# The last token block's schedule, resident first-layer expert weights and an incremental last table in a one-layer attention and mixture-of-experts kernel

## The chip, the cores and the metric

One NeuronCore of one Trainium2 chip runs the whole kernel. The time is the device time of one execution, in microseconds; a lower time is better.

## The reference

For x of 4 sequences of 1024 tokens and 256 channels, two residual steps are computed, all in f32.

```python
x = x + attn(layernorm(x))         # causal, 16 heads of 16, ALiBi slopes, projection
x = x + ffn(layernorm(x))
# ffn: attention over the 4 sequences at each position (16 heads), h = layernorm(u + attn_out)
probs = softmax(h @ router_w.T + router_b); assign = max(top_2(probs))       # 1 of 7 experts
out = gelu(h @ w1[assign].T + b1[assign]) @ w2[assign].T + b2[assign]
ffn = layernorm(h + out)
```

Since the larger of the two best indices is taken, a token goes to one expert out of 1 to 7. The 4096 tokens are therefore sorted by expert into tiles of 128 rows, and each tile is computed with one expert's weights.

## The kernel before

`fast_layer` (line 573) writes its own order of work. There is one thread of emission; each engine then executes its instructions in the order in which they were emitted, so whatever is emitted between two steps of a chain stands between them in the queues.

**Attention.** Units of a sequence and one or two 128-token blocks run in rounds. One round scores four heads (L884 on TensorE, exp on ScalarE at L892) and weighs the values (L925). Around each pair of rounds the loop offers slots: `E_slot` for VectorE work and `D_slot` for TensorE work, in which the other coroutines may take a step. Fixed jobs are entered for a slot with `at_E` and `at_D`.

**Fronts.** A position block i of 128 positions times 4 sequences goes through `front(i, ...)` (line 1421), a generator of steps: "E" steps need VectorE, "D" steps TensorE, "P" steps wait for a step on GpSimd. Its steps are layernorm statistics (`u`), the transpose to `ut`, the q/k/v projection (L1469), the 4 x 4 scores on VectorE (`pr`, `sc`, L1490 and L1491), exp on ScalarE (L1501), `tot`, the weighted values (L1510), for the last block their sum and transpose on TensorE (`ctp`, L1533), the output projection (`ao`, L1556), the second layernorm (`rstd_h`, GpSimd, L731), the router and its choice (`hot`), the write of h to DRAM (`rows`), and the rank of each token among its expert's tokens (`place`, L1614). There are 8 fronts; fronts 6 and 7 are the last, and front 7 can start only when attention has ended.

`take_E` and `take_D` (lines 1817 and 1833) walk the list `running` (at most two fronts, plus a table builder put ahead of them) and let each take at most one E step in a slot; after an E step a D step has to wait for one slot more.

**Tables.** After six fronts `tabulate_first` sorts the first 3072 tokens into 18 full tiles. After all eight, `tabulate_rest` (line 1179) splits the ranks, counts the tokens per expert (`counts`, L1106 and L1115), finds each token's tile, spreads the last two fronts' places into one-hot tiles (`at_places`, L1099), sums them on TensorE (`who`, L1266) and writes the row numbers of the other 20 tiles.

**Tiles.** A tile (class `Tile`, line 1638) is gathered by an indirect DMA on GpSimd (L1647). Its expert's first weights, 256 KB, are loaded by a DMA on SyncE whose address comes from the table (L1663, 8 buffers). Then come three stages, one per `tile_step`: transposes and a ScalarE copy (`mtp`, L1674, `mt`, L1676); the first layer and gelu (`hid`, L1687, `ge`, L1696); the second layer, whose weights lie in SBUF whole as `w2` (`oe`, L1703 to L1708). Pairs of tiles are finished over the following steps: statistics on VectorE, `rstd_v` on GpSimd (L731), two VectorE operations a tile (L1720, L1723), and a scatter by an indirect DMA on GpSimd (L1730). PSUM holds three pairs of `oe`.

**The tail.** After attention (line 1985) the loop at line 2052 offers three E slots and one D slot in an iteration with a `tile_step` between each two. While a front is under way, `tile_step` does nothing if at most `HELD_BACK` = 6 tiles are left, or if the PE cost booked for tiles is above the VectorE cost booked.

```python
        if queue or running and part.placed < NT:
            if experts.left() <= HELD_BACK or busy["PE"] > busy["DVE"]:
                return
            busy["PE"] += TILE_PE
            busy["DVE"] += TILE_DVE
        experts.fetch()
        experts.advance()
```

Of the kernel before, what the change touches and what calls it, by code (L numbers as in the profile page):

```python
# [37 lines left out]
P = 128  # L38
# [3 lines left out]
G = H // 4  # L42
# [24 lines left out]
N_W1 = 8  # L67
HELD_BACK = 6
TILE_PE, TILE_DVE = 2.6, 1.6
# [503 lines left out]
def fast_layer(ctx: ExitStack, tc: tile.TileContext, odd, x, wq, wk, wv, wp, w_in, w_out, w_r,  # L573
# [146 lines left out]
    def norm_stats(src, n, name, tag=""):  # L720
        stats = small.tile([P, B, 6], F32, tag="stats" + tag, name=f"stats_{name}")
        mv = small.tile([P, B, 2], F32, tag="mv" + tag, name=f"mv_{name}")
        rstd = small.tile([P, B], F32, tag="rstd" + tag, name=f"rstd_{name}")
        for i in range(n):
            nc.vector.bn_stats(stats[:, i], src(i))
            nc.vector.bn_aggr(mv[:, i], stats[:, i])
        nc.vector.tensor_scalar(rstd[:, :n], mv[:, :n, 1], EPS, None, ALU.add)
        return mv, rstd

# [334 lines left out]
    class Routing:  # L1064
# [6 lines left out]
        def prepare(self):  # L1071
# [4 lines left out]
            self.firsts = numbered("firsts", [P, N_COLUMNS], [[P, N_COLUMNS]])  # L1076
# [7 lines left out]
            )  # L1084

# [18 lines left out]
        def counts(self, n):  # L1104
            pm = bank(f"counts{n}")
            nc.tensor.matmul(pm[:, :E], ones_bf, self.so_far, start=True, stop=True)  # L1106
            count = keep.tile([P, E], F32, tag="count", name=f"count{n}")
            if n == 0:

                nc.vector.tensor_scalar(count, pm[:, :E], float(P - 1), None, ALU.subtract)  # L1110
            else:
                nc.vector.tensor_copy(count, pm[:, :E])
            some = N_COLUMNS if n else len(FIRST) * B
            full = keep.tile([P, E, N_COLUMNS], F32, tag="full", name=f"full{n}")[:, :, :some]
            nc.vector.tensor_tensor(  # L1115
                full, count.unsqueeze(2).to_broadcast([P, E, some]),
                self.firsts[:, :some].unsqueeze(1).to_broadcast([P, E, some]), ALU.is_gt,
            )
            tiles = const(f"tiles{n}", [P, E])
            nc.vector.tensor_reduce(tiles, full, AX.X, ALU.add)  # L1120
            return tiles

        def own_of(self, lo, hi):
            own = keep.tile([P, N_COLUMNS, E], F32, tag="own", name=f"own{lo}")[:, lo:hi]
            nc.vector.tensor_tensor(
                own, con(IOTA, E).unsqueeze(1).to_broadcast([P, hi - lo, E]),
                self.expert.rearrange("p k t -> p (k t)")[:, lo:hi].unsqueeze(2).to_broadcast(
                    [P, hi - lo, E]
                ), ALU.is_equal,
            )  # L1130
            return own
# [22 lines left out]
        def tabulate_first(self):  # L1154
# [3 lines left out]
            self.tiles = self.counts(0)  # L1158
# [8 lines left out]
            own = self.own_of(0, n)  # L1167
# [9 lines left out]
            yield from self.tabulate(0, 0, N_FIRST, nowhere, self.past(0, N_TILES, self.until, "whose0"))  # L1177

        def tabulate_rest(self):

            yield "D", 0.3
            lo, hi = len(FIRST) * B, N_COLUMNS
            self.split(lo, hi)
            tiles = self.counts(1)
# [6 lines left out]
            nc.vector.tensor_tensor(before, until, tiles, ALU.subtract)  # L1191
            found = const("found", [P, N_COLUMNS])
            self.looked_up(found, self.own_of(0, N_COLUMNS), before, "behind_of")
            nc.vector.tensor_tensor(found, found, self.by_128, ALU.add)

            mine, tile_of = found[:, :lo], self.tile_of[:, :lo]
            nc.vector.tensor_tensor(mine, mine, tile_of, ALU.subtract)
            nc.vector.tensor_tensor(mine, mine, self.late[:, :lo], ALU.mult)
            nc.vector.tensor_tensor(mine, mine, tile_of, ALU.add)
# [14 lines left out]
        def tabulate(self, n, first, end, tile_of, whose):  # L1214
# [11 lines left out]
            if n == 0:  # L1226
# [7 lines left out]
            nc.vector.tensor_scalar(  # L1234
                in_tile[:, :, 1], in_tile[:, :, 2], row_no, None, ALU.mult
            )
# [4 lines left out]
            who = table("who_f", [P, 3, n_tiles])  # L1241
            if n == 0:
                nc.vector.memset(who, 0.0)
# [17 lines left out]
            else:  # L1261
                at_place = late["at_place"]
                self.spread(at_place[-1], len(FIRST) * B, N_COLUMNS)
# [6 lines left out]
                self.whose = whose()  # L1270
                nc.vector.tensor_copy(who, pm)
# [10 lines left out]
            block, at_t = (table(name, [P, n_tiles], I32) for name in ("block", "at_t"))  # L1282
            nc.vector.tensor_scalar(  # L1283
                who[:, 2], who[:, 2], -float(NOWHERE), float(NOWHERE), ALU.mult, ALU.add
            )
            nc.vector.tensor_tensor(who[:, 1], who[:, 1], who[:, 2], ALU.add)
# [4 lines left out]
                who[:, 1], block, float(P), who[:, 1], ALU.mult, ALU.add  # L1291
            )
            nc.vector.scalar_tensor_tensor(
                out_rows, at_t, float(T), who[:, 1], ALU.mult, ALU.add
# [126 lines left out]
    def front(i, fact, more, last):  # L1421
# [6 lines left out]
        yield "E", 0  # L1428
# [71 lines left out]
        yield "E", 0  # L1500
        nc.scalar.activation(sc, sc, AF.Exp, scale=1.0 / math.sqrt(D))  # L1501
        yield "P", 1.6
# [44 lines left out]
        if not last:  # L1547
            if i < PC * (NC - 2):
                yield "E", 0
            yield "D", 2.4  # L1550
            ct = flipped(ctx_, "ct")
        yield "D", 1.8
        for t in range(B):
# [7 lines left out]
            nc.vector.tensor_tensor(u_[:, t], u_[:, t], pm, ALU.add)  # L1561
            if t == 1:
                yield "d", 1.8
        yield "E", 2.6

        taken = small.tile([P, B, E], F32, tag="taken", name=f"taken_{i}", bufs=2)
        nc.vector.tensor_copy(taken, u_[:, :, C:])
        mv, rstd = norm_stats(lambda t: u[:, t], B, f"h_{i}")
        yield "E", 0
# [36 lines left out]
        yield "E", 2.2  # L1606
        nc.vector.tensor_tensor(u, u, wide(row(G1)), ALU.mult)
# [3 lines left out]

        pm = bank(f"place_{i}")
# [12 lines left out]
        nc.vector.tensor_reduce(part.rank[:, i], rank, AX.X, ALU.add)  # L1625
        here = small.tile([P, E], F32, tag="here", name=f"here_{i}")
        nc.vector.tensor_reduce(here, hot.rearrange("p t e -> p e t"), AX.X, ALU.add)
        nc.vector.tensor_tensor(part.so_far, part.so_far, here, ALU.add)
        part.placed += 1
        if part.placed == len(FIRST):  # L1630
            running.insert(0, Running(part.tabulate_first()))
        if part.placed == NT:
            running.insert(0, Running(part.tabulate_rest()))
# [4 lines left out]
    class Tile:  # L1638
# [14 lines left out]
        def load_w1(self):  # L1653

            at = nc.values_load(
                self.table.at_w[0:1, self.j:self.j + 1], engines=[mybir.EngineType.SP],
# [6 lines left out]
            nc.sync.dma_start(  # L1663
                self.w1.rearrange("p c f -> p (c f)"),
                w1.rearrange("p e c f -> p (e c f)")[:, bass.ds(at + CC * C, CC * C)],
            )

        def stages(self):
# [7 lines left out]
            nc.scalar.copy(mt, pt)  # L1676
            yield
# [62 lines left out]
    class Experts:  # L1740
# [3 lines left out]
        def __init__(self):  # L1744
            self.step, self.fetched = 0, []
            self.n_fetched = self.n_finished = self.n_loaded = 0
            self.to_load = []
            self.under_way, self.done, self.finishing = [], [], []

        def fetch(self):  # L1750
            self.step += 1
            if tiles_to_do and self.n_fetched - self.n_finished < len(given):
# [4 lines left out]
                self.to_load.append(t)  # L1757
            while late and self.to_load and self.n_loaded - late["n_hid"] < N_W1:
                self.to_load.pop(0).load_w1()
                self.n_loaded += 1  # L1760
# [5 lines left out]
        def advance(self):  # L1766
            for it in list(self.finishing):
                n, stages = it
                if next(stages, self) is self:
                    self.finishing.remove(it)  # L1770
                    self.n_finished += n
# [384 lines left out]
```

## Time and profile before

| | us |
|---|---|
| median of 3 runs (869.72 to 882.4) | 875.27 |
| the profiled execution | 877.08 |
| its span, first to last instruction | 875.3 |
| TensorE busy in the span | 767.9 |
| VectorE busy | 535.7 |
| ScalarE busy | 393.1 |
| GpSimd busy | 253.1 |
| mean granted TensorE clock | 0.931 |

The span is on the profile's own clock, and 1.8 us of the execution lie outside it. A busy share is a mean over stages; the stages have different limits, so the stretches of the span have to be read one by one. "Idle before" an instruction is the engine's idle time ahead of it, with what ended it.

### The profile page before, as it was taken

Reading aid. Unit: us, or ns where it says so; the run is one execution under the profiler, and the core shown is the slowest. Engines: PE = TensorE matmul, PEld = TensorE weight load, DVE = VectorE, ACT = ScalarE, POOL = GpSimd, SP = SyncE. Lnnn points to the kernel's source line nnn. Section 1 sums busy time; section 2 is a strip of 40 time slices with the busy share of each in tenths; the row PEclk is TensorE's granted clock in tenths of the full one; section 3 lists DMA queues with packets and bytes.
Section 4 is the critical chain, followed back from the end, with each engine's and each line's share of the span. In section 5 each row is a group of like instructions: output and inputs, shape, how many; then the busy total and the mean of one; then the engine's idle time right before and its main releaser. Section 6 shows DMA issues by size and latency. Waiting matters only on the chain.

```text
span 875.3 us, 22574 instructions
## 1 busy us (share of the span) xinstructions
PE 767.9 (88%) x8981; PEld 576.8 (66%) x8981; DVE 535.7 (61%) x1275; ACT 393.1 (45%) x548; POOL 253.1 (29%) x359
## 2 busy tenths in 40 slices
PE   3998889998999999999999989989995997654993
PEld 2776667666666676666777767677773785543882
DVE  7334346339467773866687483793797668682454
ACT  1453436556555755655654554565461223100220
POOL 5432114212111211112121211121122448115685
PEclk9897979999999999999999999999996999865997
DMA  6445454524423333332554343244215563017550
GB/s 203 116 106 162 113 155 129 156 74 154 134 76 107 94 100 124 98 110 79 153 146 142 112 138 120 75 117 140 74 40 161 161 191 119 8 43 240 170 156 30
DMA packets 79108, 105.60 MB, mean 121 GB/s; under 512 B 19928, under 2 KB 59155, under 8 KB 78484
## 3 DMA queue, kind: packets, MB, share of 16 engines
q1 hardware_dynamic: 73548, 89.22, 34.7%
q0 software_dynamic: 4864, 14.16, 5.2%
q8 instruction: 73, 1.20, 0.6%
q10 hardware_dynamic: 584, 0.70, 0.3%
q14 instruction: 39, 0.32, 0.1%
HBM read 67.58 MB, written 35.12 MB: 117 GB/s over the span
## 4 chain that ended last, share of the span: by engine, by line
PE 58%; DVE 16%; issue 10%; DMA 6%; POOL 6%; ACT 2%; SPq 2%; POOLq 0%; DVEq 0%; ACTq 0%
PE sk L884 16%; PE pv L925 10%; PE qkvp L1469 8%; PE qkp L803 5%; PE op L991 3%; PE vp L824 3%; PE ao L1556 2%; DVE pv L1510 2%; POOL given L1647 2%; PE hid L1687 2%; POOL out_dram L1730 2%; PE oe L1703 2%; ACT p L892 2%; DVE pv L1543 1%; DMA yc<-y 1%
## 5 line engine op out<-in xcount | busy, mean ns | idle before, releaser
L892 ACT ACTIVATE p<-sk 128x1024 f32<-128x1024 f32 (+1 forms) x320 | 289.7, 937 | 210.2 <-PE sk L884 197.9
L902 POOL TENSOR_SCALAR_AFFINE_SELECT p<-p 128x512 f32<-128x512 f32 (+1 forms) x160 | 105.6, 663 | 453.2 <-ACT p L892 450.9
L884 PE MATMUL sk<-slots 32*128 32x128 f32 (+1 forms) x3456 | 217.8, 336 | 21.1 <-ACT p L892 16.2
L884 PEld LDWEIGHTS sk<-slots 32*128 32x128 f32 x3456 | 162.3, 191 | 77.7 <-ACT p L892 31.6
L925 PE MATMUL pv<-p,v 128*32 128x128 f32 (+1 forms) x3456 | 146.5, 318 | 0.0
L925 PEld LDWEIGHTS pv<-p,v 128*32 128x32 f32 x3456 | 98.2, 113 | 36.8 <-issue 7.8
L1469 PE MATMUL qkvp<-w_in,ut 128*128 128x512 f32 (+1 forms) x256 | 92.4, 495 | 0.2 <-DVE x L984 0.2
L803 PE MATMUL qkp<-xt,wqk 128*128 128x256 f32 x256 | 66.7, 406 | 0.7 <-ACT xt L793 0.7
L1469 PEld LDWEIGHTS qkvp<-w_in,ut 128*128 128x128 f32 x256 | 44.4, 190 | 31.1 <-issue 25.7
L803 PEld LDWEIGHTS qkp<-xt,wqk 128*128 128x128 f32 x256 | 50.2, 202 | 11.6 <-issue 2.0
L1687 PE MATMUL hid<-mt,w 128*128 128x128 f32 x304 | 49.9, 304 | 6.0 <-DMA w<-in_w_dram 3.0
L1476 DVE COPY qkv<-qkvp 128x264 f32<-128x264 f32 x28 | 12.1, 432 | 68.6 <-PE qkvp L1469 68.6
L1687 PEld LDWEIGHTS hid<-mt,w 128*128 128x128 f32 x304 | 44.2, 208 | 12.8 <-ACT mt L1676 5.6
L1647 POOL DMA_INDIRECT given<-rows,rows x38 | 42.2, 1109 | 33.2 <-DVE who_f L1283 14.4
L1696 ACT ACTIVATE ge<-hid 128x256 f32<-128x256 f32 x38 | 14.6, 383 | 82.6 <-PE hid L1691 44.2
L808 DVE COPY kq<-qkp 128x512 f32<-128x512 f32 x32 | 21.9, 686 | 46.6 <-PE qkp L803 46.3
L1478 ACT COPY qkv<-qkvp 128x512 f32<-128x512 f32 (+1 forms) x36 | 20.2, 562 | 48.5 <-PE qkvp L1469 45.2
L1510 DVE TENSOR_TENSOR pv<-qkv,sc 128x1024 f32<-128x1024 f32 x32 | 39.6, 1241 | 3.9 <-PE ctp L1533 3.7
L1703 PE MATMUL oe<-w,ge 128*128 x152 | 41.8, 400 | 0.1
L1730 POOL DMA_INDIRECT out_dram<-o,out_rows x38 | 39.4, 1037 | 6.9 <-issue 6.9
L1490 DVE TENSOR_TENSOR pr<-qkv 128x1024 f32<-128x1024 f32 x32 | 39.9, 1246 | 0.0
L991 PE MATMUL op<-wp,yc 128*128 128x256 f32 x124 | 34.6, 421 | 5.9 <-DVE yc L979 5.8
(259 smaller groups left out, 1003.9 us busy)
## 6 DMA issues: line engine op xcount, KB each, us to landing
slots<-k SPq DMA_DIRECT2D x128, 80.0 KB
w<-in_w_dram SPq DMA_DIRECT2D x38, 256.0 KB
k<-kq SPq DMA_DIRECT2D x32, 256.0 KB
y<-yt SPq DMA_DIRECT2D x24, 256.0 KB
v<-v SPq DMA_DIRECT2D x20, 288.0 KB
v<-v SPq DMA_DIRECT2D x4, 1152.0 KB
x<-in_x_dram SPq DMA_DIRECT2D x16, 256.0 KB
rows<-x SPq DMA_DIRECT2D x32, 128.0 KB
```

The lines of the kernel that those rows point to most:

```text
L803: nc.tensor.matmul(pm[:, k * W:(k + 1) * W], wqk[:, k, cc, half * P:(half + 1) * P], xt[:, cc], start=cc == 0, stop=cc == CC - 1,)
L884: nc.tensor.matmul(ps[h // 2][:, h % 2, width:to], kt[rows_, kb * P:(kb + 1) * P], qt[rows_, off:], start=True, stop=True,)
L892: nc.scalar.activation(pt[:, :, :width], ps[pair][:, :, :width], AF.Exp, scale=1.0 / math.sqrt(D))
L902: nc.gpsimd.affine_select(blocks, blocks, pattern=[[0, 2], [0, size], [1, P]], compare_op=ALU.is_ge, fill=0.0, base=0, channel_multiplier=-1,)
L925: nc.tensor.matmul(pv[h * S:(h + 1) * S, off:], vt[:, kb, at:at + S], pts[h // 2][:, h % 2, at_p:to], start=r == 0 and k == 0, stop=own an ...
L991: nc.tensor.matmul(pm[:, i * C:(i + 1) * C], yc[:, cc, i * P:(i + 1) * P], wp_sb[:, cc], start=cc == 0, stop=cc == CC - 1,)
L1469: nc.tensor.matmul(pq, ut[:, cc, t * P:(t + 1) * P], w_in_sb[:, cc, lo:hi], start=cc == 0, stop=cc == CC - 1,)
L1510: nc.vector.tensor_tensor(pr.rearrange("p s (h d) -> p s h d", d=D), qkv[:, :, 2 * C:3 * C].rearrange("p s (h d) -> p s h d", d=D), sc[:, ...
L1647: nc.gpsimd.indirect_dma_start(out=self.hx, out_offset=None, in_=t.rows_of, in_offset=bass.IndirectOffsetOnAxis(ap=t.rows_[:, self.j:self. ...
L1687: nc.tensor.matmul(ph[:, fc], self.w1[:, cc, fc * P:(fc + 1) * P], mt[:, cc], start=cc == 0, stop=False,)
L1703: nc.tensor.matmul(self.v, ge[:, fc], late["w2"][:, bass.ds(at + fc * C, C)], start=fc == 0, stop=False,)
L1730: ins = nc.gpsimd.indirect_dma_start(out=out.rearrange("t n c -> (t n) c"), out_offset=bass.IndirectOffsetOnAxis(ap=t.table.out_rows[:, t. ...
```

## The change

1. The last block's front is put at the head of `running` as `alone=True`. In the tail a coroutine takes all its E steps in a row in one slot, and front 7 may take its D step in the slot right after an E step. Steps that only issue to GpSimd or ScalarE become "N" steps, which end a row. In the last front the second layernorm's statistics are taken within the `ao` loop.
2. Tile steps are emitted by credit: each slot adds its E cost and 1.0, and a tile step costs 2.6, while more than `HELD_BACK` = 4 tiles wait and front 7 is not near its end. Two of these four are emitted, without finishing, ahead of the table, then six gathers.
3. The last four jobs of attention units of the last chunk, and the start of its fronts, are entered one or two E slots earlier. The last E slot of attention gives one step only. `project_slots` comes ahead of the weights' loads.
4. `w1` is loaded whole (1.75 MB, like `w2`) once; `copy_w1` reads the tile's expert number into a ScalarE register and copies 128 x 512 f32 from SBUF to SBUF on ScalarE, into 3 buffers.
5. `counts_all` is computed beside the last `place`; tiles per expert come from a shift instead of a comparison with 32 thresholds; `prepare_rest` does the part of the last table that concerns fronts 0 to 6 ahead of time; `in_tile`'s row plane is made by ScalarE.

```diff
-N_W1 = 8
-HELD_BACK = 6
-TILE_PE, TILE_DVE = 2.6, 1.6
+N_W1 = 3
+HELD_BACK = 4
+TILE_PE, STEP = 2.6, 1.0
...
+        def count_all(self, hot):
+            self.all = bank("counts_all")[:, :E]
+            for k, of_one in enumerate([self.so_far] + [hot[:, t] for t in range(B)]):
+                nc.tensor.matmul(self.all, ones_bf, of_one, start=k == 0, stop=k == B)
...
+        def prepare_rest(self, stage):
+
+            n = len(FIRST) * B
+            if stage == 0:
+
+                tile_of, late_ = self.tile_of[:, :n], self.late[:, :n]
+                nc.vector.tensor_tensor(
+                    self.own[:, :n], self.own[:, :n],
+                    late_.unsqueeze(2).to_broadcast([P, n, E]), ALU.mult,
+                )
+                by = const("by_late", [P, n])
+                nc.vector.tensor_tensor(by, self.by_128[:, :n], tile_of, ALU.subtract)
+                nc.vector.tensor_tensor(by, by, late_, ALU.mult)
+                nc.vector.tensor_tensor(tile_of, tile_of, by, ALU.add)
+            else:
+                self.split(n, n + B)
+                self.found_first(n, n + B)
+                nc.vector.tensor_copy(self.tile_of[:, n:n + B], self.by_128[:, n:n + B])
+                self.spread(late["at_place"][-1][:, :B], n, n + B)
 
         def tabulate_rest(self):
 
-            yield "D", 0.3
-            lo, hi = len(FIRST) * B, N_COLUMNS
+            lo, hi = N_COLUMNS - B, N_COLUMNS
+            whole = keep.tile([P, E], I32, tag="count", name="whole_all")
+            nc.vector.tensor_scalar(whole, self.all, float(P - 1), None, ALU.add)
+            nc.vector.tensor_single_scalar(whole, whole, 7, op=ALU.logical_shift_right)
+            tiles = const("tiles1", [P, E])
+            nc.vector.tensor_copy(tiles, whole)
             self.split(lo, hi)
-            tiles = self.counts(1)
...
-        def load_w1(self):
+        def copy_w1(self):
 
             at = nc.values_load(
-                self.table.at_w[0:1, self.j:self.j + 1], engines=[mybir.EngineType.SP],
+                self.table.at_w[0:1, self.j:self.j + 1], engines=[mybir.EngineType.Activation],
...
-            nc.sync.dma_start(
-                self.w1.rearrange("p c f -> p (c f)"),
-                w1.rearrange("p e c f -> p (e c f)")[:, bass.ds(at + CC * C, CC * C)],
+            nc.scalar.copy(
+                self.w1.rearrange("p c f -> p (c f)"), late["w1"][:, bass.ds(at, CC * C)]
             )
...
             nc.scalar.copy(mt, pt)
+            self.copy_w1()
             yield
...
-            if it.kind in ("E", "P") and it.slot < slot[0] - (it.kind == "P"):
+            was = it.slot
+            while it.kind in ("E", "N", "P") and was < slot[0] - (it.kind == "P"):
                 if cost and cost + it.cost > most:
-                    continue
+                    break
...
+                if it.kind != "E" or not (it.alone or most > E_SLOT):
+                    break
...
-                    if it.slot >= slot[0] - (it.was == "E"):
+                    if it.slot >= slot[0] - (it.was == "E" and not it.alone):
...
-    w2_sb = const("w2", [P, E - 1, CC, C], into=tail)
-    for g in range(2, G):
-        normalise(g)
-    load_sums(last_unit)
-    for lo, hi in ((1, 3), (3, 5), (5, E)):
-        nc.sync.dma_start(w2_sb[:, lo - 1:hi - 1], w2[:, lo:hi])
+    w1_sb, w2_sb = (const(name, [P, E - 1, CC, C], into=tail) for name in ("w1", "w2"))
+    for sb, src in ((w1_sb, w1), (w2_sb, w2)):
+        for lo, hi in ((1, 3), (3, 5), (5, E)):
+            nc.sync.dma_start(sb[:, lo - 1:hi - 1], src[:, lo:hi])
...
-    queue.append(front(NT - 1, fact, 1, True))
+    fetching.clear()
+    running.insert(0, Running(front(NT - 1, fact, 1, True), True))
...
+    def tile_step(finish=True):
+        experts.fetch()
+        experts.advance(finish)
...
+    while queue or running:
+        for take in (lambda: E_slot(k, 99.0), lambda: 0.0 * D_slot(p, 99.0)):
+            credit = min(credit, TILE_PE - STEP) + take() + STEP
+            while credit >= TILE_PE and experts.waiting() > HELD_BACK and "near" not in held:
+                tile_step()
+                credit -= TILE_PE
+        if part.placed == NT - 1 and not prepared:
+            prepared = True
+            part.prepare_rest(1)
+        k, p = k + 1, p + 1
+    for _ in range(HELD_BACK // 2):
+        tile_step(False)
+    for _ in part.tabulate_rest():
+        pass
+    for _ in range(6):
+        experts.fetch()
+    n = 0
+    while experts.left():
         tile_step()
```

## The prediction

> **What bounds the kernel now.** I read the page's slices first, to find where TensorE stops being busy.
>
> ```profile
> PE   3998889998999999999999989989995997654993
> DVE  7334346339467773866687483793797668682454
> PEclk9897979999999999999999999999996999865997
> ```
>
> Attention ends in slice 31 (656.7 us). Up to there TensorE is full; after it come holes with a lowered clock. The busy time by stretches sizes them (first pair: length and TensorE busy; then weight load, DVE, ACT, POOL, clock, DMA share, GB/s):
>
> ```profile
> 740.00:760.00 20.00, 13.70 (x86) 12.45 (x85) 12.80 (x24) 1.49 (x4) 3.55 (x6) 0.83 0.09 27
> 760.00:780.00 20.00, 9.85 (x49) 8.33 (x49) 15.76 (x54) 3.21 (x7) 6.45 (x11) 0.74 0.15 50
> 780.00:800.00 20.00, 4.97 (x45) 4.07 (x45) 12.16 (x43) 0.76 (x2) 8.99 (x13) 0.53 0.38 120
> 840.00:860.00 20.00, 19.86 (x136) 17.33 (x135) 11.98 (x36) 4.37 (x13) 16.46 (x26) 1.00 0.34 101
> ```
>
> In these three stretches before 800 TensorE idles 31 us of 60: no tile is left, and nothing can be gathered until the last table is there. So the chain of front 7 and of the table sets the time. The timeline gives its landmarks:
>
> ```profile
> 672.20 0.42 DVE L725 BATCH_NORM_STATS2 stats_u<-x 128x6 f32<-128x256 f32 x1
> ...
> 696.12 1.02 PE L1469 MATMUL qkvp<-w_in,ut 128*128 128x512 f32 x2
> ...
> 713.30 1.22 DVE L1490 TENSOR_TENSOR pr<-qkv 128x1024 f32<-128x1024 f32 x1
> ...
> 743.10 0.57 DVE L1504 TENSOR_REDUCE tot<-sc 128x64 f32<-128x256 f32 x1
> ...
> 762.64 1.01 POOL L731 TENSOR_TENSOR rstd_h<-rstd_h,minus_half 128x4 f32<-128x4 f32 x1 [18.65 <-DVE rstd_h L727]
> ...
> 789.89 1.09 POOL L1647 DMA_INDIRECT given<-rows,rows  x1 [9.34 <-DVE at_t L1288]
> ```
>
> The chain takes 672.2 to 789.9; its own operations are about 70 of these 118 us, the rest is other fronts' and tiles' work ahead of it. From the first gather of the last table to the end of the span another 85.4 us pass. There GpSimd's timeline is full:
>
> ```profile
> 840.47 1.03 POOL L1730 DMA_INDIRECT out_dram<-o,out_rows  x1 [0.18 <-issue]
> 841.50 0.11 POOL L1729 MEMSET spare<- 128x1 f32 x1
> 841.80 1.00 POOL L1730 DMA_INDIRECT out_dram<-o,out_rows  x1 [0.19 <-issue]
> 843.11 1.06 POOL L1647 DMA_INDIRECT given<-rows,rows  x1 [0.30 <-issue]
> 844.19 0.74 POOL L731 TENSOR_TENSOR rstd_v<-rstd_v,minus_half 128x2 f32<-128x2 f32 x1
> ```
>
> With its gaps a gather or a scatter costs it 1.31, an rstd 0.92; two tiles 6.2 (840.47 to 846.71), so 3.1 a tile against TensorE's 2.69 (849.77, 852.46, 855.14: the starts of oe).
>
> **What the Trainium skill says.** "ScalarE: Activation LUTs", What ACT_TABLE_LOAD costs: an ACTIVATE without pointer operands takes 186 ns + 0.833 ns an element, a table load 1283 ns. The trace agrees: 0.37 for 256 elements (formula 0.40), 1.28 for the loads at L1501. "DMA: Bandwidth & Descriptors", SWDGE vs HWDGE vs iDMA: for a DMA issued from GpSimd a core of GpSimd computes the descriptors; the 1.0 to 1.3 us per issue above agree. The same page, Latency and other measured facts, puts tensor_load's floor at about 600 ns; TensorE's queue shows 302 ns for the same register load, and that is used. "TensorE: Matmul & The Clock Gate", What's actually happening: an idle window of about 3.4 us halves the clock; four hid matmuls took 1.19 at 768.77, after a hole, and 0.61 in the full stretch at 851.17.
>
> **The change, part by part.**
>
> *Start of front 7.* Before, VectorE did ahead of its statistics, after 658.1: at_place 1.75, two weighted values 2 x 2.3, yn 2.5, x and yc 1.25, the first table 2.6, and a wait of 1.3. Now one E step at most (1.75), yc and two x 1.25, yn 2.5, TensorE's wait 1.3: start at about 664, 8 earlier. The rest isn't gone; it lies behind the statistics: one weighted value and the table, 4.9, delay the shift to 671.3.
>
> *To q/k/v.* norm_apply on ScalarE 2.07, ut 1.0 and its copies 1.1: 675.5. On TensorE front 6's ao (4.3) and two young tile steps (2) are ahead: q/k/v starts at 681 (before 696). In a row it is 4 x 2.8 = 11.2; before, tile steps stretched it to 17. With the last copy: 693, 20 earlier.
>
> *Scores and softmax.* One block on VectorE: 0.2 + 4 x 2.44 + 1.0 = 11.0, ends at 704 (before 21). Meanwhile credit (11 for front 7, 7.7 for front 6's router) releases about 8 tile steps, 21.5 of TensorE: hidden, but exp waits behind their ScalarE work to about 714, plus 1.7 with the table load. VectorE also has front 6's router, 8.6, and three pairs' finish, 8.1, ahead of tot: tot at 721 (before 743). Here the row gives back what it won: 17 from block to tot, before 9.
>
> *tot to rank.* tot and weighted 12.8 as before, plus a pair's finish in between, so 14.5: 735.5. ao to rank before 755.9 to 771.1, 15.2; three of four statistics now lie under ao (-1.9), a scatter may stand before rstd_h on GpSimd (+1.3): 750.
>
> *Last table.* Before, 771.1 to 789.9: 8.6 of tile finishes ahead and 10.2 of table. The finishes are gone (`finish=False`). From the table go full and tiles 0.84, half of spread 0.6, found 0.36, own and count 0.5; ScalarE's plane (0.72 by the skill's formula) lies beside in_tile's 0.82. 8.4 remains: first gather at 758.5, 31.4 earlier. prepare_rest and three spreads, 6.4 of VectorE, are hidden under TensorE's ctp and ao; uncovered they'd cost that.
>
> *w1.* On SyncE 38 loads go (the last 20 took 44.1 of its queue, paced by buffers); three of about 0.5 each come ahead of front 7's row writes: hidden. 1.75 MB at the 193 GB/s of 660 to 680 take 9: landed at about 670, before the first copy (about 677). On ScalarE each tile adds a register load, 0.3, and a copy, 0.61, behind mt (0.37): with 0.2 of signalling 1.5 from mtp's end, under the 1.89 of the older tile's oe. Cost 0; without that cover (first tiles) about 1.0 each. Bounds for a tile: -0.1 (no DMA wait: 3.0 us of it in all before) to +1.0; taken 0. Behind a waiting copy stand ge and front 7's evictions, and TensorE's hid waits for it.
>
> *The end.* After the table GpSimd owes 20 gathers, 30 scatters (only 8 of 38 are emitted before) and 14 rstd: 50 x 1.31 + 14 x 0.92 = 78.4, and 7.1 from the last issue (868.2) to the span's end: 85.5. TensorE alone would need 22 x 2.69 + 4 + 15 = 78; but with three oe pairs it may lead rstd_v by four steps only, so the order of GpSimd decides: 85 (before 85.4, then 24 scatters and 10 of idling). Nothing is won here.
>
> *Sum.* 758.5 + 85 = 843.5 of span against 875.3. The profiled execution (877.08) lies 0.2% over the median, outside the span is 1.8: forecast 844.
>
> **Rivals.** 2% (about what a measurement of this kernel can tell) lies at 857.8 and 892.8.
> 1. *VectorE takes the chain's lead away.* It has some 74 us of work in the 94 up to the table, in order; a pair's statistics emitted ahead of front 7's next step wait for TensorE. Two such waits of a q/k/v block (11 each) leave a lead of about 10: 866. For: tot's 17 above. Against: tiles' finishes come four steps after their start.
> 2. *The ScalarE copy becomes the tile's bound (slower).* If load and copy hold ScalarE for long, each step is mtp to hid. The lead of 31.4 is used up and 17.5 added when 36 steps lengthen by 1.36: from a chain of 1.89 + 1.36 = 3.25, that is 2.65 for load and copy instead of 0.91. At 3.5: 900. Against: the same register load takes 0.3 on TensorE, four ACTIVATEs from SBUF 2.07.
> 3. *More is won.* Front 6's router falls under the q/k/v row (-8.6), and GpSimd's backlog is smaller, the end 78 to 80: 828 and less, 822 with both in full.
> 4. *The change doesn't do what it says:* table not earlier, 875; it has a part in rival 1.
>
> **How the numbers follow.** Forecast 0.58, 844, own range 832 to 857; rival 1 (with 4) 0.20, 858 to 885; rival 2 0.10, over 893; rival 3 0.12, 815 to 832. Faster 0.70, same 0.20, slower 0.10. The range 820 to 868 leaves out rival 2, the upper half of rival 1 and the edge of rival 3.
>
> **What would show it.** Right: front 7's q/k/v is one piece of about 11 us from 681, tot near 721, the first gather of the last table near 758, then 85 us with GpSimd busy over 80%, and TensorE's idle time between 740 and 800 gone. Wrong: hid waiting for `w1` or for ScalarE in every tile (rival 2); tot after 735 or stats_v waiting for oe in front of it (rival 1); a gap under 80 us from that gather to the end (rival 3).

## The result and the profile after

The kernel after takes 885.15 us (median of 20 runs) against 876.55 for the kernel before (20 runs beside it): ratio 1.0116, 95% interval 1.0088 to 1.0143. I had forecast 844. It is slower by 1.2%, some 10 us by the ratio (the medians lie 8.6 apart), not faster by 31. Its profiled execution has a span of 884.5 us and a mean granted clock of 0.936.

The slices of the page, to be laid beside those of before:

```profile
PE   3978889999999999999899979889984995658993
DVE  7414336329557774866866493966496269584553
PEclk9988979999999999999899999979997898888997
```

The holes of TensorE behind slice 30 are still there. In slice 32 (685.5 to 707.6) TensorE has a 9 and VectorE a 2, before a 6: TensorE does tiles there, while VectorE stands almost still where front 7 should be under way. The busy time by stretches (first pair: length and TensorE busy):

```profile
740.00:760.00 20.00, 10.35 (x69) 9.17 (x68) 14.74 (x40) 5.17 (x11) 12.08 (x15) 0.83 0.35 111
760.00:780.00 20.00, 9.38 (x53) 8.44 (x54) 13.41 (x44) 2.82 (x6) 1.04 (x1) 0.85 0.01 1
780.00:800.00 20.00, 14.91 (x110) 12.45 (x109) 16.20 (x59) 5.71 (x13) 6.59 (x7) 0.81 0.31 93
```

TensorE idles 25 of these 60 us (31 before). The timeline gives the same landmarks as before:

```profile
673.06 0.42 DVE L728 BATCH_NORM_STATS2 stats_u<-x 128x6 f32<-128x256 f32 x1
...
709.62 1.02 PE L1519 MATMUL qkvp<-w_in,ut 128*128 128x512 f32 x2
...
721.21 1.22 DVE L1540 TENSOR_TENSOR pr<-qkv 128x1024 f32<-128x1024 f32 x1
...
751.05 0.57 DVE L1554 TENSOR_REDUCE tot<-sc 128x64 f32<-128x256 f32 x1
...
774.82 1.04 POOL L743 TENSOR_TENSOR rstd_h<-rstd_h,minus_half 128x4 f32<-128x4 f32 x1 [18.69 <-DVE taken L1626]
...
791.58 1.09 POOL L1709 DMA_INDIRECT given<-rows,rows  x1 [15.72 <-PE hid L1753]
```

Read against the prediction: q/k/v starts at 709.6, not 681 (before 696.1), and the last table's first gather is at 791.6, not 758.5 (before 789.9). The row (front 7's E steps in one slot) does there what I said: from q/k/v's start to the first pr 11.6 us. What comes between statistics and q/k/v is not: 36 us, I had 17. Its first half is one chain through four engines:

```profile
683.77 0.62 ACT L1725 COPY w<-w 128x512 f32 x1 [10.33 <-DMA w<-in_w_dram]
684.44 1.22 PE L1749 MATMUL hid<-mt,w 128*128 128x128 f32 x4 [11.54 <-ACT w L1725]
...
693.00 1.04 PE L1498 MATMUL ctp<-ident,ctx 128*128 128x128 f32 x8
694.08 0.69 DVE L1502 COPY ct<-ctp 128x512 f32<-128x512 f32 x1 [13.96 <-PE ctp L1498]
694.68 0.15 DVE L750 SCALAR_TENSOR_TENSOR shift_u<-mv_u,rstd_u 128x4 f32<-128x4 f32 x1
```

The first copy of an expert's weights waits 10.3 for the load; TensorE's first hidden layer waits for the copy; two tiles and an oe stand on TensorE ahead of front 6's flip (`ctp`, the transpose of its weighted values); VectorE waits 14.0 for the flip; and front 7's shift is queued behind that copy on VectorE, though its statistics were done at 675.3 and the root that it needs (`rstd_u`, on GpSimd behind seven gathers) at 678.7. I read six tiles' hidden layers on TensorE between 684.4 and q/k/v's start.

### The profile page after: what moved, and what is told of

It is laid out like the page before. It is cut to its first block, busy times and chain, and to the rows that moved or that the text cites. A ratio compares the mean times of both kernels' runs of the same rounds, so it can differ in the third digit from the quotient of the medians.

```text
span 884.5 us, 22510 instructions
## 1 busy us (share of the span) xinstructions
PE 766.0 (87%) x8985; PEld 575.2 (65%) x8985; DVE 536.8 (61%) x1281; ACT 416.0 (47%) x587; POOL 248.1 (28%) x359
## 5 line engine op out<-in xcount | busy, mean ns | idle before, releaser
L896 PE MATMUL sk<-slots 32*128 32x128 f32 (+1 forms) x3456 | 215.1, 336 | 24.0 <-ACT p L904 15.2
L914 POOL TENSOR_SCALAR_AFFINE_SELECT p<-p 128x512 f32<-128x512 f32 (+1 forms) x160 | 101.0, 634 | 469.7 <-ACT p L904 467.3
L937 PE MATMUL pv<-p,v 128*32 128x128 f32 (+1 forms) x3456 | 148.7, 322 | 0.0
L815 PEld LDWEIGHTS qkp<-xt,wqk 128*128 128x128 f32 x256 | 50.4, 203 | 11.6 <-issue 2.0
L1541 DVE TENSOR_REDUCE sc<-pr 128x64 f32<-128x1024 f32 x32 | 39.0, 1220 | 1.1
```

The costliest lines, as they stand in the source:

```text
L815: nc.tensor.matmul(pm[:, k * W:(k + 1) * W], wqk[:, k, cc, half * P:(half + 1) * P], xt[:, cc], start=cc == 0, stop=cc == CC - 1,)
L896: nc.tensor.matmul(ps[h // 2][:, h % 2, width:to], kt[rows_, kb * P:(kb + 1) * P], qt[rows_, off:], start=True, stop=True,)
L914: nc.gpsimd.affine_select(blocks, blocks, pattern=[[0, 2], [0, size], [1, P]], compare_op=ALU.is_ge, fill=0.0, base=0, channel_multiplier=-1,)
L937: nc.tensor.matmul(pv[h * S:(h + 1) * S, off:], vt[:, kb, at:at + S], pts[h // 2][:, h % 2, at_p:to], start=r == 0 and k == 0, stop=own an ...
L1541: nc.vector.tensor_reduce(sc[:, t], pr.rearrange("p s (h d) -> p s h d", d=D), AX.X, ALU.add)
```

## Experiments

All ratios are to the kernel before on the same chip, with the 95% interval. My first theory: the loads stand too late in SyncE's queue, and the attention ends later because of its moved slots. Rivals: the copy costs in every tile; VectorE's order.

**Loads first.** The pools and the six loads move up directly behind the attention's end, ahead of the divisions and of `load_sums`.

```diff
     attention.close()
+    tail, work, ps_x = ...
+    for sb, src in ((w1_sb, w1), (w2_sb, w2)): ...
     for what in of_E.pop(k, ()):
```

> The kernel after, with the six loads of the experts' weights issued by SyncE directly behind the end of the attention, ahead of the two divisions of the last block, of its sums' load and of its projection; nothing else moves. Theory (the loads stand too late in SyncE's queue, and the first ScalarE copy that waits for them blocks ScalarE, then TensorE, then VectorE): the loads start about 4 us earlier (668.7 instead of 672.75), the copy's wait of 10.3 us shrinks to about 6, front 7's shift comes about 4 earlier, and the time falls from 885 to about 881. Rival (the copies cost ScalarE time in every tile, the first wait is hidden): no change, 885. Rival (VectorE's order is the cause): the shift moves earlier, but the rank of the last place doesn't, 885.

Measured 1.0125 (1.0078 to 1.0172), as without the edit. The loads did start earlier (669.35, before that 672.75), but:

```profile
678.93 0.62 ACT L1725 COPY w<-w 128x512 f32 x1 [3.43 <-DMA w<-in_w_dram]
...
687.98 2.04 PE L1765 MATMUL oe<-w,ge 128*128 x4 [1.59 <-DMA w<-in_w_dram]
...
692.63 0.69 DVE L1502 COPY ct<-ctp 128x512 f32<-128x512 f32 x1 [10.42 <-PE ctp L1498]
```

The copy's wait falls from 10.3 to 3.4 and VectorE's only from 14.0 to 10.4: the tile steps ahead of the flip now wait for the table load of gelu, for the next copies and for the second weights. So one late load is not all of it; whole tile steps stand in the wrong place.

**Slots before.** The attention's slots as before, the tail as changed.

```diff
-            soon = c == NC - 1
+            soon = u == last_unit - 1
-                if it.kind != "E" or not (it.alone or most > E_SLOT):
+                if it.kind != "E" or not (it.alone or most > E_LATE):
-        E_slot(2 * p + 1, most if p < len(rounds) // 2 - 1 else 0.0)
+        E_slot(2 * p + 1, most)
```

> The kernel after, with the attention's slots of before: load of sums, inversion, load of y, division and projection of each unit of the last chunk but the last one at 3, 5, 6, 9 and 5 again instead of 2, 4, 5, 8 and 4; no row of E stages in one slot before the attention's end; the last slot takes E stages again. The tail is that of after. Theory (TensorE, in order, meets a projection whose quotient isn't there yet, and several E stages in one slot delay the exponentials): the last exponential starts at about 654 to 656 again instead of 664.9, everything behind it comes 8 to 10 us earlier, and the time is about 876. Rival (the attention's end is late for another reason, such as the clock of this one execution): the last exponential stays at 663 or later and the time within 3 us of 885.

Measured 0.9979 (0.9947 to 1.0011): 1.4% of the kernel's time comes back. The shift is at 680.5 and q/k/v at 692.6, with one tile ahead of it:

```profile
680.46 0.15 DVE L750 SCALAR_TENSOR_TENSOR shift_u<-mv_u,rstd_u 128x4 f32<-128x4 f32 x1
...
692.55 1.02 PE L1519 MATMUL qkvp<-w_in,ut 128*128 128x512 f32 x2
```

**Both.** 

> Both edits, the loads first and the slots of before, in the kernel after. Theory: the two gains stand in a row on the same chain, so they add: 885 - 9 - 4 = 872, faster than the kernel before. Rival: once the attention ends early, the first tile waits for gathered rows or for VectorE instead, and the sum is less than either alone, about 880.

Measured 0.9970 (0.9946 to 0.9994): the loads' place adds nothing here either.

**Copy alone.** The kernel before, with w1 loaded once and ScalarE's copy in place of the per-tile load.

```diff
             nc.scalar.copy(mt, pt)
+            self.copy_w1()
             yield
```

> The kernel before with one part of the change: the experts' first weights are loaded once (three loads behind the last sums, ahead of the second weights'), and ScalarE copies each tile's out of them behind its transposes' copy; three buffers instead of eight; no per-tile load. Theory (a copy of 0.62 us in a tile step of 2.7 is covered; only the first wait counts): the first hidden layer waits until the loads land, some 6 to 8 us later than the 676.2 of before, of which front 7 hides a part: 878 to 884. Rival (the copy becomes the bound of each tile): 30 tiles by some 0.5 us, about 890 or more. Rival (the part costs nothing and frees SyncE and the DMA queues): 872 to 876.

Measured 1.0008 (0.9984 to 1.0032). The copy costs nothing that shows; rival 2 of the prediction falls.

**Which half of the slots.** First only the earlier projection is taken back ("soon off"), then only the rows of E stages ahead of the attention's end, together with the idle last slot ("rows off").

> The changed kernel with one half of the slots of before: the last chunk's units load their sums, invert, load y, divide and project one slot later, as before; rows of E stages in the last attention slots and the idle last slot stay as changed. Theory for the share of each half: TensorE waited 6.2 us for quotients in the changed kernel against 1.5 before, which the later slots take away, so of the 12 us that both halves together brought, this half brings 4 to 6 (ratio to before about 1.007). Rival (the whole cost is the earlier projection): ratio 0.998 as with both. Rival (the whole cost is the rows of E stages): ratio 1.012 as with neither.

Measured 1.0135 (1.0087 to 1.0183).

> The changed kernel with the other half of the slots of before: no row of E stages in one slot before the attention's end, and the last slot takes E stages again; the last chunk's projections stay one slot earlier, as changed. After 'soon off' the theory is that the rows alone delay the attention: the last exponential starts at 655 to 658 and the ratio to before is 0.996 to 1.000, as with both halves. Rival (it takes both halves): ratio 1.010 or more.

Measured 0.9998 (0.9976 to 1.0020). My share for the projection was wrong: taking it back brings nothing that shows, and the rows, with the idle slot, are all of it, 1.2% or 10 us. I had read the condition `most > E_SLOT` as one for the tail, but the last chunk's slots, with E_LATE = 3.6, meet it too: fronts take their E steps in rows while attention still runs. The first table is then ready within the attention, so that its tiles are at hand when the tail begins. Its row numbers, in the kernel after and in rows off:

```profile
658.78 0.18 DVE L1343 SCALAR_TENSOR_TENSOR out_rows<-at_t,out_f 128x18 int32<-128x18 int32 x1
```

```profile
678.90 0.18 DVE L1343 SCALAR_TENSOR_TENSOR out_rows<-at_t,out_f 128x18 int32<-128x18 int32 x1
```

**No row in the tail.** Slots before, and front 7 queued like the other fronts, one stage a slot.

```diff
-    running.insert(0, Running(front(NT - 1, fact, 1, True), True))
+    queue.append(front(NT - 1, fact, 1, True))
```

> The changed kernel with the attention's slots of before and without the row after the attention's end: the last front is queued as the others are, and each slot takes one of its stages, as in the kernel before. Theory (front 7 and front 6 share VectorE, so the row only moves the wait from ahead of the products pr to ahead of tot, and the last place's rank comes at 771 either way): the rank within 3 us of 770.6, the ratio to before 0.995 to 1.003. Rival (the prediction's steps: the row wins some 10 us on the chain to the rank): rank at 780 or later and ratio about 1.008.

Measured 1.0094 (1.0058 to 1.0130), the rank's end at 781.6. My theory fell and the prediction's step stood: the row, with the place at the head of the list, wins 28.0 us at pr (732.2 to 704.1), 19.7 at tot and 11.0 at the rank. VectorE's timeline of slots before shows where the part that is lost again goes:

```profile
713.81 0.58 DVE L1548 TENSOR_REDUCE top<-sc 128x64 f32<-128x256 f32 x1
...
719.58 1.22 DVE L1112 TENSOR_TENSOR at_places<-places,left 128x1024 bf16<-128x1024 f32 x1
720.72 1.38 DVE L759 TENSOR_SCALAR u<-u,mv_h,rstd_h 128x256 f32<-128x256 f32 x4
...
735.62 0.57 DVE L1554 TENSOR_REDUCE tot<-sc 128x64 f32<-128x256 f32 x1
```

From 714.8 to 735.6 VectorE works almost without a pause on other things: finishing pairs (4.8, later 6.7), a spread (1.2) and front 6's norm and router (8.2).

**Table later.** Slots before, plus six repetitions of the final check of the sums on VectorE ahead of the last table.

```diff
+    for _ in range(6):
+        check_sums()
     for _ in part.tabulate_rest():
```

> The changed kernel with the attention's slots of before (the run 'slots before' gave 877.9 beside 879.3 for the kernel before), and VectorE made busy with six repetitions of the final check of the sums (0.42 + 0.69 + 0.69 + 0.16 us each, about 11.5 us together, same result each time) between the last place's rank and the last table: the table's gain of 10.5 us is taken back by hand, all else stays. Theory (the time after the table's first gather is set by GpSimd's and TensorE's remaining work, which an earlier table only stretches; the table's end is not what sets the end): the first gather of the last table comes 11 later, the time rises by 0 to 4 us. Rival (the table's end is on the path, and what it won was lost elsewhere): the time rises by 10 to 11 us.

Measured 1.0063 (1.0034 to 1.0093): 0.84% or 7.4 us more than slots before, without these checks. Between the two: an 11.5 us later table costs about two thirds of itself (the two intervals leave some 4 us either way). In the profiles the first gather comes 9.3 later, and the tail, from there to the last scatter, shrinks from 88.0 to 81.2. So the table's gain is real, but a part of it is lost in the tail.

That is not a matter of when the tail starts. Nine kernels have the tail of after, with six gathers and the deferred pairs. In soon off, hold (below) and table later it takes 81.2 to 81.4, from first gathers at 796.5, 781.2 and 788.4; in loads first, slots before, both, rows off and no row it takes 88.0 to 88.7, from first gathers at 777.0 to 791.1; in the kernel after 84.8. What goes with it is TensorE's longest wait for ScalarE's copy of weights in the tail: 3.4 to 4.2 us in the five of 88, 1.5 in the kernel after, none over 0.9 in the three of 81. Ahead of it ScalarE starts a gelu late, though its hidden layer is done, and the profile names no engine that it waited for. In slots before that hidden layer was done at 800.8:

```profile
804.50 0.38 ACT L1758 ACTIVATE ge<-hid 128x256 f32<-128x256 f32 x1 [5.04 <-remote]
...
806.33 1.22 PE L1749 MATMUL hid<-mt,w 128*128 128x128 f32 x4 [3.87 <-ACT w L1725]
```

What ScalarE waits for there stays open.

**The tail's start.** In the kernel after, GpSimd's timeline and then the waits of 785 to 815 (total, times, longest):

```profile
799.57 1.01 POOL L1709 DMA_INDIRECT given<-rows,rows  x1 [0.30 <-issue]
800.60 0.73 POOL L743 TENSOR_TENSOR rstd_v<-rstd_v,minus_half 128x2 f32<-128x2 f32 x1
```

```profile
PE oe L1765 <- DVE o L1782: 6.0, 2, 3.3
DVE o L1785 <- issue: 3.5, 1, 3.5
```

Seven gathers (791.58 to 800.58) stand in GpSimd's queue ahead of the first pair's root (`rstd_v`); VectorE's o, which needs the root, has 3.5 of idle time before it (the view names no engine for it, but it ends as the root does). TensorE, whose oe has no free bank, waits for o twice, 6.0 in all, and the second wait, of 3.3, ends behind this root. Two edits to slots before: finish pairs in the two steps ahead of the table ("finish before"), and two gathers instead of six behind it ("two gathers").

```diff
-        tile_step(False)
+        tile_step()
```

> The changed kernel with the attention's slots of before, and the two tile steps ahead of the last table also finish pairs (statistics, the two operations of o, the scatters), as all other steps do. Theory (the tail is slow to start because two finished pairs and their scatters are deferred behind the table: o and GpSimd's queue are then late, and TensorE waits for the banks of oe): the table comes 3 to 5 us later, GpSimd has up to 4 scatters of 1.3 us less behind it, TensorE's waits of 5.9 us for o at 780 to 795 go, and the time falls by 2 to 5 us against 'slots before' (ratio to before about 0.994). Rival (deferral is harmless, the table's time is what counts): 3 to 5 us slower than 'slots before', ratio about 1.003.

Measured 0.9931 (0.9906 to 0.9955). The table takes 2.8 longer, the tail falls from 88.0 to 75.6.

```diff
-    for _ in range(6):
+    for _ in range(2):
         experts.fetch()
```

> The changed kernel with the attention's slots of before, and two gathers instead of six in a row behind the last table; the others come one in each tile step. Theory (seven gathers of 1.3 us stand in GpSimd's queue ahead of the first pair's root, so VectorE's o waits 3.5 us and TensorE's oe waits behind it): the root comes 5 us earlier, TensorE starts again about 4 us earlier, and the time falls by 3 to 5 us against 'slots before'. Rival (the gathers' number is what bounds, wherever they stand): the time stays within 1.5 us; second rival (the first tiles of the last table then wait for their rows): 2 to 5 us slower.

Measured 0.9880 (0.9822 to 0.9937), 1.0% below slots before and more than I expected. The tail falls to 79.5. The root comes at 780.0, behind three gathers:

```profile
777.99 1.01 POOL L1709 DMA_INDIRECT given<-rows,rows  x1 [0.30 <-issue]
779.98 0.71 POOL L743 TENSOR_TENSOR rstd_v<-rstd_v,minus_half 128x2 f32<-128x2 f32 x1 [0.97 <-DVE rstd_v L733]
```

**Both tail edits**, with the earlier projection taken back ("tail") and without ("tail with rows off").

> The changed kernel with the attention's slots of before, the pairs finished ahead of the last table, and two gathers instead of six behind it. Theory (both take the same backlog off GpSimd and VectorE where TensorE starts on the last 20 tiles, so they add only in part): ratio to before 0.980 to 0.986, below each alone (0.993 and 0.988). Rival (each already removed the one wait): ratio 0.987 to 0.989.

Measured 0.9880 (0.9839 to 0.9922): the rival's number holds. Two gathers alone had brought as much, and finishing ahead of the table adds nothing to them.

> The same with the last chunk's projections one slot earlier, as the change has them: only the rows of E stages ahead of the attention's end, the deferred finishing and the six gathers are taken back. Theory (the earlier projections are worth little either way): within 0.3% of the run 'tail'. Rival (they win the 1 to 2 us that the earlier end of the last units is worth): 0.2 to 0.4% faster than it.

Measured 0.9892 (0.9846 to 0.9937): no difference from the earlier projection.

**Hold.** How do rows inside the attention cost 10 us? The order of TensorE's instructions gave the idea: with the rows two tiles' hidden layers stand ahead of front 6's flip, without them none. The kernel after, with no tile step before front 7's norm:

```diff
         norm_apply(..., f"u_{i}", scalar=last)
+        if last:
+            held.pop("near")
...
     fetching.clear()
+    held["near"] = True
```

> The changed kernel, rows of E stages and all, with one thing held back: no tile step before front 7's norm is issued, so that front 6's flip stands ahead of the first tile's hidden layer on TensorE. Theory (the rows cost 12 us because two tile steps, which wait for the experts' weights, got ahead of front 6's flip, for which VectorE and so front 7's shift waits): the shift comes at about 680 to 683 instead of 694.7 although the attention ends as late as before (last exponential at 664 to 668), and the ratio to before falls from 1.012 to 0.998 to 1.003. Rival (the attention's late end costs the time): the ratio stays at 1.008 to 1.014.

Measured 1.0021 (1.0005 to 1.0037), 0.95% less than the kernel after, with the rows in place. The flip doesn't wait for tiles, and the shift follows it, 6.9 us behind the end of the statistics instead of 19.4:

```profile
675.34 1.33 PE L1500 MATMUL ctp<-ident,ctx 128*128 128x128 f32 x5 [1.88 <-DVE ctx L1596]
...
677.31 0.20 DVE L750 SCALAR_TENSOR_TENSOR shift_u<-mv_u,rstd_u 128x4 f32<-128x4 f32 x1
...
686.96 0.61 PE L1751 MATMUL hid<-mt,w 128*128 128x128 f32 x4
```

In this profile the attention happened to end early (last exponential at 658.4), so the shift's place alone would say little. In the next run's profile the attention ends as late as in the kernel after (665.2), and the shift is at 682.7, again 6.9 behind the statistics.

**Hold and two gathers** ("hold, two").

> The same hold, and two gathers instead of six in a row behind the last table. Theory (the two losses lie at different places, ahead of the rank and behind the table, and add): ratio 0.985 to 0.991. Rival: 0.995 or more.

Measured 1.0009 (0.9989 to 1.0029): expectation missed, almost nothing is added. The profiles show in which kernel the difference lies: with two gathers the tail takes 79.3 to 79.5 with the rows and without, but with six it takes 81.3 with hold and 88.0 in slots before, whose late gelu is shown above.

**Hold, two gathers, loads first** ("hold, first, two").

> Hold, two gathers, and the experts' weights loaded first. Theory (with the hold the first copy still meets weights that land at 683.7 and stands ahead of front 7's flip copies on ScalarE; loads issued 4 us earlier take that away): 2 to 4 us below the run 'hold, two gathers'. Rival (the loads are hidden there): the same within 1.5 us.

Measured 1.0002 (0.9977 to 1.0028): loads hidden, the rival holds.

**The same with rows off.**

> Hold, two gathers, loads first, and no rows of E stages ahead of the attention's end. Theory (without the rows the first tiles come behind front 6's flip by themselves, so hold and loads bring nothing more): the ratio of the run 'tail', 0.988, within 0.3%. Rival (the earlier loads let tiles run in front 7's gaps): 0.980 to 0.984.

Measured 0.9867 (0.9839 to 0.9896), as the tail runs. But it differs from the run before it by the rows (and the idle slot) alone, and by 1.35%. So the hold had not found all of what the rows do. TensorE in the kernel with rows ("hold, first, two"), from front 6's last ao to q/k/v:

```profile
690.80 0.61 PE L1751 MATMUL hid<-mt,w 128*128 128x128 f32 x4
...
693.39 0.71 PE L1751 MATMUL hid<-mt,w 128*128 128x128 f32 x4 [1.14 <-ACT w L1727]
...
696.33 0.71 PE L1751 MATMUL hid<-mt,w 128*128 128x128 f32 x4
...
699.13 1.02 PE L1521 MATMUL qkvp<-w_in,ut 128*128 128x512 f32 x2
```

and in the one without:

```profile
692.11 0.38 PE L1737 MATMUL mtp<-ident,given 128*128 128x128 f32 x2
692.32 1.02 PE L1521 MATMUL qkvp<-w_in,ut 128*128 128x512 f32 x2
```

Three tile steps, 8.3 us, still stood ahead of q/k/v; and their pairs are then finished on VectorE ahead of tot (four pairs' o instead of two). From the statistics to the rank the two profiles differ by 16.5, of which 9.1 lie ahead of q/k/v and 7.1 between the first pr and tot; the tails are alike (79.4 and 79.5). That it is these three steps is read from the timelines; no run moved them alone. Read for all versions, from front 7's last statistics to the last place's rank:

| tiles ahead of q/k/v on TensorE | versions | statistics to rank, us |
|---|---|---|
| 6 | after, loads first, soon off | 108.0, 105.3, 109.1 |
| 3 | hold; "hold, two"; "hold, first, two" | 102.4, 102.2, 103.5 |
| 1 | slots before, both, rows off, table later, finish before, two gathers, tail, tail with rows off | 93.4 to 96.2 |
| 0 | "hold, first, two" with rows off, and the two below | 87.0 to 88.5 |
| 5, no row | before; copy alone; no row | 96.6, 97.2, 100.6 |

Among the versions with the row the chain grows with the tiles ahead. The last line has another order of VectorE's work and is no part of this.

**The fastest versions**: hold, loads first, no rows in the attention, two gathers, pairs finished ahead of the table, and then the same with eight buffers for o.

> Hold, loads first, no rows ahead of the attention's end, two gathers, and pairs finished ahead of the last table. Theory (the two pairs deferred behind the table keep four scatters of 1.3 us in GpSimd's queue, for which o and then oe wait): 2 to 5 us below the version without the last edit (0.987), so 0.981 to 0.985. Rival (the finish ahead delays the table by as much as it saves, as the run 'tail' against 'two gathers'): 0.985 to 0.989.

Measured 0.9852 (0.9798 to 0.9906).

> The same with eight buffers for o instead of four. Theory (o's waits of 16.3 us for the scatters' landing pass on to TensorE only where oe has no free bank, about 6 us at the start): 0 to 3 us faster than with four. Rival (GpSimd's own rate of 6.2 us for two tiles sets the tail, buffers only move the wait): within 1 us.

Measured 0.9821 (0.9773 to 0.9870), 860.5 us beside 876.9: faster than both kernels. The two intervals overlap too much to price the last edit or the four buffers.

## Why the prediction was wrong

The sum, term by term, of the prediction and of the kernel after:

| term | predicted | measured |
|---|---|---|
| front 7's statistics start | 664.0 | 673.1 |
| to its shift | 7.3 | 21.6 |
| to q/k/v's start | 9.7 | 14.9 |
| to the first pr | 12.0 | 11.6 |
| to tot | 28.0 | 29.8 |
| to the rank's end | 29.0 | 32.0 |
| to the last table's first gather | 8.5 | 8.5 |
| to the span's end | 85.0 | 92.9 |
| sum | 843.5 | 884.5 |

The step that failed is the way from front 7's statistics to q/k/v. Ahead of the shift I put "one weighted value and the table, 4.9", and ahead of q/k/v, on TensorE, front 6's ao and "two young tile steps (2)". There were six tile steps on TensorE, and two of them, and an oe, stood even ahead of front 6's flip, for which the shift waits in VectorE's order. That cost 14.3 ahead of the shift and 5.2 behind it, the late weights included: 19.5 of the 41 us missed. In the profile of rows off these two terms are 7.9 and 11.6, close to what I had predicted (7.3 and 9.7). Rows off (1.2%) and hold (0.95%, with the rows in place) price it. I had counted what the row takes off VectorE and not asked what the credit would put on TensorE in the meantime. Two things come together: the rows inside the attention bring the first table forward by 20 us, so that tiles are at hand, and in the tail every slot's E cost fills the credit that releases them.

*w1* was mis-sized, but isn't the cause. I let it land at about 670; it was issued at 672.75 behind `load_sums` and landed at 683.8. In these 11 us the loads' queue moved 2.42 MB, w1's part of it and some of w2's, and the gathers of the first table, which I had not counted, another 1.20. Moving the loads gave nothing, with the tile steps in their place (1.0125) or held back (1.0002). Its other half was right: a copy takes 0.62 (the Trainium skill's formula for an ACTIVATE, "ScalarE: Activation LUTs", What ACT_TABLE_LOAD costs, gave 0.61), the register load shows no gap (mt at 727.57 for 0.37, the copy at 727.94), a tile step takes 2.74 against 2.69, and the run copy alone prices the part at 0.1%, within its interval of nothing.

*Start of front 7* was wrong in its base, not in its length. From the last copy of yt to the statistics 4.5 us pass (before 15.4; I had 7.3), but the attention's end, which I took as given, lies at 668.6 in this execution (before 656.8). How much of that the change causes isn't settled. In four other executions with the same attention program the last exponential starts at 658.4 to 665.4 (after 664.9), and in soon off at 668.2; in the twelve changed kernels without the rows it starts at 655.4 to 665.7. The means, 664.1 with rows and 659.1 without, suggest some 5 us for the rows.

*Scores and softmax* and *tot to rank*: the block of 11 us and "here the row gives back what it won" were right, and the run no row prices the row, with the place at the head of the list, at 1.15%. tot to rank was 3 short: front 6's place, its preparation for the table and two spreads lie between the weighted values.

*Last table*: 8.5 as predicted, and the table's gain of 10.5 counts only in part (table later).

*The end* was mis-sized by 8: I counted GpSimd's work, 85, and not its order. With the six gathers ahead of the first root, TensorE starts badly on the last 20 tiles; finishing pairs ahead of the table (0.5%) or two gathers (1.0%) win that back in slots before.

Of the rivals the nearest was rival 1 in kind, VectorE's order holding up front 7; its sign, tot after 735, came (751.1), and its range, 858 to 885, ends just at the measured time. But that is luck in the number: its waits of 11 were foreseen for pairs' statistics, and it came to 866. Rival 2, the only one that was slower than before, was the wrong mechanism. The slow outcome that I should have written down is the one above: the tiles' credit overtakes the front.

What stays open: how much later the attention itself ends because of the rows, and why ScalarE starts a gelu late in the five kernels whose tail takes 88 us. With two gathers no gelu is that late. The tail is where two gathers bring 1.0% without the rows and only 0.1% with rows and hold; no run tried the late gelu by itself. Nor does the best version reach the forecast: 860.5 against 844.

## What to carry to other kernels

When several streams of work share engines that run in order, and a counter releases one of the streams, don't only cost the stream that is moved up: list what the counter now releases ahead of its next step on each engine, and count those instructions with their waits. A condition meant for one stage (here `most > E_SLOT`) has to be checked against every call that can meet it. And a gain on the chain need not arrive at the end: behind it, look at what stands in each queue ahead of the first thing that frees a buffer.

## What the runs showed of the hardware

- ScalarE copies 128x512 from a place given by a register in 0.62 us, 38 times, without a visible gap for the register's load. The kernel before with such copies takes the time that it takes with 38 loads by DMA (ratio 1.0008, 0.9984 to 1.0032).
- The six loads of the experts' weights (four of 512 KB, two of 768 KB) took 11 us from the first issue to the first copy that needed the first three, while gathers ran beside them; issuing them 3.4 earlier brought that copy 4.8 forward.
- The same attention program, profiled once in each of five kernels, ended as much as 7 us apart. A landmark's shift of that size between two single profiles is no finding.
